# The last eight slots laid out along TensorE's list, a second exponential tile, and one-by-one projects for the last four batches

## The chip, the cores and the metric

One core of one Trainium2 chip. The time is the device time of one launch in microseconds; a number for a kernel is the median of its runs. All runs told here are of the state fast. The kernel before takes 2411.36 us (median of 4, 2406.54 to 2418.76), so differences of a few us in 2400 are near the scatter between runs. I therefore also use a length inside one trace, the **tail**: from the start of the attend of batch 116 on TensorE to the end of the span. Up to that attend the order of work is the same in all kernels here (some have one extra transfer shortly before); where it starts moved between 2250 and 2268 us from trace to trace. The tail itself repeated within 0.5 us in the two kernels that were traced twice. But in the traces of runs b, e and h one stretch of it ran at the lower clock after a gap that the other traces with list and tile passed at full pace, and the tail is about 2 us longer for it (shown under run b). So for an edit that acts only near the end I also count from the start of the attend of batch 124 on TensorE.

## The reference, cut to what matters

Two layers over x of 128 batches x 128 rows x 512 columns, all float32. The change concerns the end of the second:

```python
qkv = (h @ w_qkv)                                   # h = relu(layernorm(x))
attn = softmax(where(mask == 0, -inf, q @ k.T * scale))
o = (attn @ v) @ w_proj + b_proj
x = x + o + (layernorm(o) * gamma + beta)           # per row of 512
```

## The kernel before: the parts concerned

All work of a batch is put on a heap with a time in us on a plan of slots (17.8 us a batch), then built in order of these times. Each engine executes its instructions in that order. So a time in the plan is only a rank: it decides who stands behind whom.

```python
def softmax_exp(i, t, s, shift):
    e = work.tile([P, Q, H, R], F32, name="e", bufs=1)         # one tile for all batches
    sm = stat.tile([P, H], F32, name="sm")
    ...                                                        # 8 exponentials on ScalarE, in two halves
    put(t + 4.2, softmax_divide, i, t + 4.2, e, sm)

def softmax_divide(i, t, e, sm):
    nc.vector.reciprocal(sm, sm)
    nc.gpsimd.tensor_tensor(e, e, sm..., op=ALU.mult)
    S[i] = work.tile([P, Q, H * R], F32, name="sx", bufs=1)    # where it comes back
    exchange(max(t + 5, read_at(i)), S[i], e...)               # to DRAM and back, then a transpose

def finish_last(i, n, x1):
    nc.gpsimd.tensor_tensor(n, n, x1, op=ALU.add)
    nc.sync.dma_start(out=out[i], in_=n)                       # same SP queue as the exchanges
```

The qkv product (four batches at once) and the project (two at once) are done with 7 products in place of 8: "Q" and "p" below are one step of each. The factors for them are sums made on GpSimd (osum, hsum). A finish of a batch is: statistics on VectorE, a power on GpSimd (rs), a shift on VectorE, the normalization on ScalarE, then two more 128x512 instructions on GpSimd besides an add of the residual, and a store.

In the old plan the last batches follow rules of distance: scores of the last four 8.5 us apart, attend 22 us later, seven project steps 1.4 us apart after that.

## Time and profile before

| | before |
|---|---|
| median | 2411.36 us |
| tail | 154.0 us (2257.7 to 2411.7) |

What TensorE does in this tail is taken apart in the prediction. In the waits' view a line reads: engine, its line of the kernel, what released it, then us in total, times, longest. One line that the prediction leans on and does not show, from ScalarE's waits in the tail of the kernel before:

```profile
ACT e L409 <- DMA d<-e: 15.1, 3, 8.4
```

The exponentials waited 15.1 us in three places for their tile to leave for DRAM.

### The profile page before, as it was taken

What the parts mean: (1) busy time and instruction counts of PE and PEld (TensorE: products, weight loads), DVE (VectorE), ACT (ScalarE), POOL (GpSimd) and SP (SyncE); (2) the same over time, 40 slices, a digit from 0 to 9 for tenths busy, and PEclk for the clock granted to TensorE, in tenths of its full rate; (3) what the DMA queues carried; (4) which work ended last, traced back from release to release, by engine and by line L of the source; (5) the groups of instructions that cost most, each with busy time, mean ns of one, the idle gap of its engine ahead of it and who ended that gap; (6) DMA issues with size and microseconds to landing.
All of it is one profiled execution on the core that took longest, in us unless ns stands there. A gap on an engine that the chain in (4) does not pass through costs nothing.

```text
span 2411.7 us, 42673 instructions
## 1 busy us (share of the span) xinstructions
PE 2341.9 (97%) x14097; PEld 2052.3 (85%) x14097; DVE 1612.0 (67%) x3231; ACT 1044.3 (43%) x3074; POOL 1677.9 (70%) x1598
## 2 busy tenths in 40 slices
PE   7899999999999999999999999999999999999985
PEld 6788888888888888888888888888888888888873
DVE  5566676676676776676676676676676666766554
ACT  2344444444444444444444444444444444444332
POOL 4467677677677677677777677767777766776556
PEclk9999999999999999999999999999999999999997
DMA  7776766766766776767776776776766767676643
GB/s 233 237 230 217 231 216 215 236 218 214 232 218 220 225 223 220 225 209 227 224 226 215 231 222 206 229 221 214 235 216 218 226 209 226 218 220 212 219 153 105
DMA packets 399788, 524.10 MB, mean 217 GB/s; under 512 B 40016, under 2 KB 250064, under 8 KB 399568
## 3 DMA queue, kind: packets, MB, share of 16 engines
q1 hardware_dynamic: 398192, 519.99, 67.7%
q8 instruction: 113, 1.85, 0.3%
q10 hardware_dynamic: 1376, 1.38, 0.2%
q14 instruction: 107, 0.88, 0.1%
HBM read 350.29 MB, written 170.92 MB: 216 GB/s over the span
## 4 chain that ended last, share of the span: by engine, by line
PE 84%; DMA 5%; POOL 3%; DVE 3%; issue 2%; SPq 2%; ACT 1%; POOLq 0%; DVEq 0%; ACTq 0%
PE pc L366 37%; PE pd L286 23%; PE pz L366 6%; PE ps L386 5%; PE po L433 5%; PE pmix L272 4%; PE pz L286 4%; DMA sx<-d 2%; SPq L211 1%; DMA wq<-wt 1%; DVE pT L424 1%; POOL x1b L454 1%; POOL t L460 1%; POOL t L464 1%; DMA wq<-in_L_gnn_w_qkv_dram 1%
## 5 line engine op out<-in xcount | busy, mean ns | idle before, releaser
L193 POOL TENSOR_TENSOR rs<-ve,minus_half 128x2 f32<-128x2 f32 x192 | 134.9, 703 | 630.1 <-DVE ve L191 550.5
L366 PE MATMUL pc<-hsum,wq 128*128 128x256 f32 x2048 | 487.0, 381 | 16.2 <-ACT qkT L370 5.0
L409 ACT ACTIVATE e<-s,mx 128x128 f32<-128x128 f32 x1024 | 397.0, 389 | 194.7 <-DVE mx L400 113.2
L366 PEld LDWEIGHTS pc<-hsum,wq 128*128 128x128 f32 x2048 | 390.1, 191 | 73.6 <-ACT qkT L370 7.7
L286 PE MATMUL pd<-wp_sb,osum 128*128 128x256 f32 x1024 | 266.4, 384 | 6.9 <-DVE o L292 3.6
L418 POOL TENSOR_TENSOR e<-e,sm 128x1024 f32<-128x1024 f32 x128 | 244.9, 1913 | 36.0 <-DVE sm L417 30.7
L366 PE MATMUL pc<-h1T,wq 128*128 128x256 f32 x1024 | 246.4, 384 | 0.6 <-DMA wq<-in_L_gnn_w_qkv_dram 0.6
L286 PE MATMUL pd<-w_sb,ysum 128*128 128x256 f32 x960 | 246.3, 379 | 0.0
L366 PE MATMUL pc<-wq,hsum 128*128 128x256 f32 x1024 | 244.6, 382 | 0.0
L614 ACT COPY oT<-po 128x512 f32<-128x512 f32 x128 | 74.9, 585 | 385.2 <-PE po L433 385.2
L424 DVE STREAM_TRANSPOSE pT<-sx 128x1024 f32<-128x1024 f32 x128 | 158.5, 1238 | 124.5 <-DMA sx<-d 124.5
L286 PEld LDWEIGHTS pd<-wp_sb,osum 128*128 128x128 f32 x1024 | 191.8, 193 | 33.4 <-POOL osum L220 5.5
L366 PEld LDWEIGHTS pc<-h1T,wq 128*128 128x128 f32 x1024 | 192.9, 191 | 30.4 <-DMA wq<-in_L_gnn_w_qkv_dram 0.7
L366 PEld LDWEIGHTS pc<-wq,hsum 128*128 128x128 f32 x1024 | 191.8, 190 | 28.8
L394 DVE TENSOR_TENSOR s<-ps,maskb 128x512 f32<-128x512 f32 x256 | 159.2, 684 | 57.6 <-PE ps L386 57.6
L286 PEld LDWEIGHTS pd<-w_sb,ysum 128*128 128x128 f32 x960 | 177.9, 190 | 21.7
L370 ACT COPY qkT<-pc 128x512 f32<-128x512 f32 x256 | 144.1, 574 | 119.3 <-PE pc L366 119.1
L459 ACT ACTIVATE t<-o,shift,rs 128x512 f32<-128x512 f32 x128 | 103.1, 807 | 207.0 <-DVE shift L197 206.0
L409 ACT ACTIVATION_READ_ACCUMULATOR e<-s,mx 128x1 f32 x1024 | 191.6, 187 | 0.0
L454 POOL TENSOR_TENSOR x1b<-x1b,o 128x512 f32<-128x512 f32 x128 | 162.7, 1271 | 35.5 <-DMA x1b<-x1d 33.4
L292 DVE TENSOR_TENSOR o<-pd,bp_b 128x256 f32<-128x256 f32 x256 | 106.3, 415 | 108.1 <-PE pd L286 107.7
L188 DVE BATCH_NORM_STATS2 st<-x 128x6 f32<-128x512 f32 x256 | 172.1, 672 | 3.0 <-DMA x<-in_x_dram 2.9
(93 smaller groups left out, 4711.7 us busy)
## 6 DMA issues: line engine op xcount, KB each, us to landing
wq<-wt SPq DMA_DIRECT2D x384, 256.0 KB, 3.8
wq<-in_L_gnn_w_qkv_dram SPq DMA_DIRECT2D x288, 256.0 KB, 3.5
d<-e SPq DMA_DIRECT2D x128, 512.0 KB, 2.9
sx<-d SPq DMA_DIRECT2D x512, 128.0 KB, 2.9
x<-in_x_dram SPq DMA_DIRECT2D x128, 256.0 KB, 4.3
d<-h SPq DMA_DIRECT2D x128, 256.0 KB, 2.9
x1d<-x SPq DMA_DIRECT2D x128, 256.0 KB, 3.1
h1x<-d SPq DMA_DIRECT2D x512, 64.0 KB, 2.3
```

The costliest lines, as they stand in the source:

```text
L188: nc.vector.bn_stats(st, src)
L193: nc.gpsimd.tensor_tensor(rs, ve, minus_half, op=ALU.pow)
L286: nc.tensor.matmul(p[:, 0, :], lhsT=left[k][:, c, :], rhs=w_sb[:, k, c, :], start=first and c == 0, stop=last and c == 1, skip_group_check ...
L366: nc.tensor.matmul(p[:, half, :], lhsT=lhsT, rhs=rhs, start=first and half == 0 and c == 0, stop=last and c == 1, skip_group_check=True)
L370: nc.scalar.copy(results[n], p)
L386: nc.tensor.matmul(ps[e][:, c, :], lhsT=qk[r, c, j % 2, :], rhs=qk[r, C + c, j % 2, :], start=True, stop=True)
L394: nc.vector.tensor_tensor(s[:, e * C:(e + 1) * C, :], ps[e], m4, op=ALU.add)
L409: nc.scalar.activation(e[:, :, h, :], s[:, h, :].rearrange("p (q r) -> p q r", q=Q), AF.Exp, bias=shift[:, h:h + 1], scale=scale, accum_ou ...
L418: nc.gpsimd.tensor_tensor(e, e, sm.unsqueeze(1).unsqueeze(3).to_broadcast([P, Q, H, R]), op=ALU.mult)
L424: nc.vector.transpose(PT[i].rearrange("p h (q r) -> p q h r", q=Q), S.pop(i).rearrange("p q (h r) -> p q h r", h=H))
L433: nc.tensor.matmul(p[e * HD:(e + 1) * HD, c, :], lhsT=v[:, h:h + HD], rhs=PT[i][:, e * C + c, :], start=True, stop=True)
L454: put(t + 1 + 3 * n, lambda i=i: nc.gpsimd.tensor_tensor(X1B[i], X1B[i], O[i], op=ALU.add))
```

## The change

Its intent: let TensorE's list of the last eight slots be written down as a string (a = attend, s = scores, Q, p = steps, D = one whole project), let all other times follow from it, bring the softmaxes closer together, give odd batches a second tile for the exponentials and the way back (a free h1T buffer), and project the last four batches one by one, which needs no sums. The residual of the last eight batches is also reloaded into the six input tiles, which are free by then (not in the cut below).

```diff
+    def spare(i):
+        return i > LATE and i % 2
+    def late(n):                                  # two halves of one free h1T buffer
+        ...
     def softmax_exp(i, t, s, shift):
-        e = work.tile([P, Q, H, R], F32, name="e", bufs=1)
+        e = late(0) if spare(i) else work.tile([P, Q, H * R], F32, name="e", bufs=1)
...
-        S[i] = work.tile([P, Q, H * R], F32, name="sx", bufs=1)
+        S[i] = late(1) if spare(i) else work.tile([P, Q, H * R], F32, name="sx", bufs=1)
...
+    def project_whole(i, t):                      # 8 matmul calls, no factor sums
+        p = whole(OT, i, lambda row, col: wp_b12 if (row, col) == (0, 1) else wp_sb[...])
...
+    LATE = LAST - G
+    for key in ("aassQQpQpQpQpQppQp" "aassQQpQpQpQpQppQpQQQQQ" "aassQpQppQp" "aassppQp" "QpQppQpppp"
+                "aaD" "aaDDD"):
+        AT[key].append(t)
+        t += dict(a=0.9, s=0.9, Q=1.73, p=0.87, D=3.46)[key]
...
     def softmax_at(i):
+        return TAIL + (5, 13, 26, 35, 58, 63.5, 70.5, 76)[i - LATE]
     def read_at(i):
+        return TAIL + (16, 24, 37, 46, 69, 74.5, 81.5, 87)[i - LATE]
...
+    put(when(LATE - 1, 6), nc.sync.dma_start, wp_b12, block(w_proj, 0, F))
```

More of the change, by code (lines that the diff above doesn't have):

```diff
@@ L68 @@
     ctx.enter_context(tc.manual_schedule())
+    LATER = []
     X, H0, YT, X1, X1D, H1, H1T, WQ, QKT, V, S, PT, OT, O, X1B, LEFT0, LEFT1, LEFT2 = ({} for _ in range(18))
@@ L179, in make_mask, with stats_of @@
         nc.vector.tensor_scalar(maskb, edge, some, None, op0=ALU.add)
-    def stats_of(pair):
-        mv = stat.tile([P, 2, nc.vector.BN_AGGR_DIM], F32, name="mv")
-        for n, src in enumerate(pair):
+    def stats_of(srcs):
+        w = len(srcs)
+        mv = stat.tile([P, 2, nc.vector.BN_AGGR_DIM], F32, name="mv")[:, :w]
+        for n, src in enumerate(srcs):
             st = stat.tile([P, nc.vector.BN_STATS_DIM], F32, name="st")
@@ L189, in stats_of @@
             nc.vector.bn_aggr(mv[:, n], st)
-        ve = stat.tile([P, 2], F32, name="ve")
+        ve = stat.tile([P, 2], F32, name="ve")[:, :w]
         nc.vector.tensor_scalar(ve, mv[:, :, 1], EPS, None, op0=ALU.add)
-        rs = stat.tile([P, 2], F32, name="rs")
-        nc.gpsimd.tensor_tensor(rs, ve, minus_half, op=ALU.pow)
-        shift = stat.tile([P, 2], F32, name="shift")
+        rs = stat.tile([P, 2], F32, name="rs")[:, :w]
+        nc.gpsimd.tensor_tensor(rs, ve, minus_half[:, :w], op=ALU.pow)
+        shift = stat.tile([P, 2], F32, name="shift")[:, :w]
         def shifts():
             nc.vector.scalar_tensor_tensor(shift, mv[:, :, 0], -1.0, rs, op0=ALU.mult, op1=ALU.mult)
-        return shifts, [dict(bias=shift[:, n:n + 1], scale=rs[:, n:n + 1]) for n in range(2)]
+        return shifts, [dict(bias=shift[:, n:n + 1], scale=rs[:, n:n + 1]) for n in range(w)]
     def exchange(t, dst, src):
@@ L296, in layer0_whole @@
     def layer0_whole(i, t):
-        p = psum.tile([P, 2, F], F32, tag=f"d{i % 2}", name=f"pd{i % 2}", bufs=1)
-        y = YT[i // 2] if i % 2 == 0 else YT.pop(i // 2)
-        for c in range(C):
-            for col in range(2):
-                nc.tensor.matmul(p[:, col, :], lhsT=y[:, c, i % 2, :], rhs=w0_sb[:, BLOCKS[c // 2][col], c % 2, :],
-                                 start=c == 0 and col == 0, stop=c == C - 1, skip_group_check=True)
+        p = whole(YT, i, lambda row, col: w0_sb[:, BLOCKS[row][col]])
         X1[i] = work.tile([P, D], F32, name="x1", bufs=3)
-        put(t + 3.6, lambda: nc.vector.tensor_tensor(X1[i], p.rearrange("p a f -> p (a f)"), X.pop(i), op=ALU.add))
+        put(t + 3.6, nc.vector.tensor_tensor, X1[i], p, X.pop(i), ALU.add)
     def layer0(j):
@@ L401, in softmax_max @@
         put(t + 1.4, softmax_exp, i, t + 1.4, s, mx)
+    def spare(i):
+        return i > LATE and i % 2
+    def late(n):
+        if not LATER:
+            t = work.tile([P, C, G, P], F32, name="h1T").rearrange("p (n c) j m -> p n (c j m)", n=2)
+            LATER.extend(t[:, n].rearrange("p (q w) -> p q w", q=Q) for n in range(2))
+        return LATER[n]
     def softmax_exp(i, t, s, shift):
-        e = work.tile([P, Q, H, R], F32, name="e", bufs=1)
+        e = late(0) if spare(i) else work.tile([P, Q, H * R], F32, name="e", bufs=1)
+        e = e.rearrange("p q (h r) -> p q h r", h=H)
         sm = stat.tile([P, H], F32, name="sm")
@@ L443, in project, with whole, finish @@
         return pair_chain(LEFT2.pop(j), wp_sb, (O[2 * j], O[2 * j + 1]), (bp_b, bp_b), "d1", "d0")
+    def whole(src, i, rhs):
+        p = psum.tile([P, 2, F], F32, tag=f"d{i % 2}", name=f"pd{i % 2}", bufs=1)
+        y = src[i // 2] if i % 2 == 0 else src.pop(i // 2)
+        for c in range(C):
+            for col in range(2):
+                nc.tensor.matmul(p[:, col, :], lhsT=y[:, c, i % 2, :], rhs=rhs(c // 2, col)[:, c % 2, :],
+                                 start=c == 0 and col == 0, stop=c == C - 1, skip_group_check=True)
+        return p.rearrange("p a f -> p (a f)")
+    def project_whole(i, t):
+        p = whole(OT, i, lambda row, col: wp_b12 if (row, col) == (0, 1) else wp_sb[:, BLOCKS[row][col]])
+        O[i] = work.tile([P, D], F32, name="o", bufs=4)
+        put(t + 3.6, nc.vector.tensor_tensor, O[i], p, bp_b, ALU.add)
     def reload(i):
-        X1B[i] = work.tile([P, D], F32, name="x1b", bufs=2)
+        X1B[i] = work.tile([P, D], F32, name="x", bufs=6) if i >= LATE else work.tile([P, D], F32, name="x1b", bufs=2)
         nc.sync.dma_start(out=X1B[i], in_=X1D.pop(i))
-    def finish(j, t):
-        pair = 2 * j, 2 * j + 1
-        shifts, args = stats_of([O[i] for i in pair])
+    def finish(batches, t):
+        shifts, args = stats_of([O[i] for i in batches])
         put(t + 3, shifts)
-        for n, (i, arg) in enumerate(zip(pair, args)):
+        for n, (i, arg) in enumerate(zip(batches, args)):
             put(t + 1 + 3 * n, lambda i=i: nc.gpsimd.tensor_tensor(X1B[i], X1B[i], O[i], op=ALU.add))
@@ L506, in run @@
             put(t, step, t, k)
+    LATE = LAST - G
+    AT = {key: [] for key in "asQpD"}
+    t, last = when(LATE, 0), ""
+    for key in ("aassQQpQpQpQpQppQp" "aassQQpQpQpQpQppQpQQQQQ" "aassQpQppQp" "aassppQp" "QpQppQpppp"
+                "aaD" "aaDDD"):
+        AT[key].append(t)
+        t += dict(a=0.9, s=0.9, Q=1.73, p=0.87, D=3.46)[key]
+        t += 0.2 * (key != last and "a" in (key, last) or key != last and "s" in (key, last))
+        last = key
+    TAIL = when(LATE, 0)
     def scores_at(i):
-        if i < LAST:
-            return when(i - i % 2, 2 + i % 2)
-        return when(LAST, 2) + (i - LAST) * 8.5
+        return when(i - i % 2, 2 + i % 2) if i < LATE else AT["s"][i - LATE]
     def softmax_at(i):
-        if i < LAST and i % 2:
-            return when(i, 0.5)
-        return scores_at(i) + 3
+        if i < LATE:
+            return when(i, 0.5) if i % 2 else scores_at(i) + 3
+        return TAIL + (5, 13, 26, 35, 58, 63.5, 70.5, 76)[i - LATE]
     def read_at(i):
-        return when(i + 1, 9) if i < LAST and i % 2 else 0
+        if i < LATE:
+            return when(i + 1, 9) if i % 2 else 0
+        return TAIL + (16, 24, 37, 46, 69, 74.5, 81.5, 87)[i - LATE]
     def flip_at(i):
-        if i < LAST:
+        if i < LATE:
             return when(i + 1, 15) if i % 2 else when(i + 2, 7.4)
-        return scores_at(i) + 20.5
+        return TAIL + (27, 29.5, 56, 58, 73, 78.5, 89.3, 91)[i - LATE]
     def attend_at(i):
-        if i < LAST:
-            return when(min(i - i % 2 + 4, LAST + 1), i % 2)
-        return scores_at(i) + 22
-    def stage(t, f, n, *a, bound=B):
-        if 0 <= n < bound:
-            put(t, f, n, *a)
+        return when(i - i % 2 + 4, i % 2) if i < LATE - 4 else AT["a"][i - LATE + 4]
     PAIR = ((5.6, 8.2, 10.8, 12.5, 15.0, 15.9, 18.5), (3.2, 5.8, 8.4, 10.1, 12.7, 13.5, 16.1))
@@ L545 @@
         put(attend_at(i), attend, i, attend_at(i))
-    idle = when(LAST, 13)
     for j in range(B // 2):
@@ L572 @@
         t = attend_at(b) + 2
-        put(t, pair_left, j, t, 3.4 if i < LAST else 1, OT, LEFT2, "osum")
-        if i < LAST:
-            times = [when(i, p) for p in PAIR[1]]
-            end = when(i + 1, 1.2)
-        else:
-            times = [max(t, idle) + 1 + k * 1.4 for k in range(7)]
-            idle = times[6] + 1
-            end = times[6] + 2
-        run(lambda j=j: project(j), times)
-        put(end - 7, reload, a)
-        put(end - 4, reload, b)
-        put(end, finish, j, end)
+        if b < LAST:
+            put(t, pair_left, j, t, 3.4 if i < LATE else 1.5, OT, LEFT2, "osum")
+            n = 7 * (a - LATE + 4) // 2
+            times = [when(i, p) for p in PAIR[1]] if i < LATE else AT["p"][n:n + 7]
+            run(lambda j=j: project(j), times)
+            ends = [((a, b), when(i + 1, 1.2) if i < LATE else times[6] + 2.2)]
+        else:
+            ends = []
+            for n in (a, b):
+                t = AT["D"][n - LAST]
+                put(t, project_whole, n, t)
+                ends.append(((n,), t + 4.6))
+        for batches, t in ends:
+            for n in batches:
+                put(t - 7 + 3 * (n % 2), reload, n)
+            put(t, finish, batches, t)
     steps = []
@@ L588 @@
         i = g * G - 3
-        t = when(i - 1, 13) if g else START + 36.2
-        put(t, group_left, g, t, 4 if g else 1.4)
+        t, gap = (START + 36.2, 1.4) if g == 0 else (when(i - 1, 13), 4) if i < LATE else (TAIL + 9.8, 2.2)
+        put(t, group_left, g, t, gap)
         times = sorted(when(i + n, p) for n in range(G) for p in GROUP[(i + n) % 2] + ((13.1,) if n == 0 else ()))
+        if i + G > LATE:
+            n = sum(t < TAIL for t in times)
+            times[n:] = AT["Q"][:5] if g == LATE // G else AT["Q"][5:]
         for kind in KINDS:
@@ L600 @@
     for kind, (t, tiles) in enumerate((
-            (START + 25, (("sx", 1, [P, Q, H * R]), ("pT", 2, [P, 2 * C, P]), ("s", 2, [P, 2 * C, P]), ("e", 1, [P, Q, H, R]))),
+            (START + 25, (("sx", 1, [P, Q, H * R]), ("pT", 2, [P, 2 * C, P]), ("s", 2, [P, 2 * C, P]), ("e", 1, [P, Q, H * R]))),
             (START + 37, (("pT", 2, [P, 2 * C, P]), ("s", 2, [P, 2 * C, P])) + (("o", 4, [P, D]),) * 4),
@@ L610 @@
     put(when(2, 12), combine_square, nc.gpsimd, wp_sb)
+    wp_b12 = w0_sb[:, 1]
+    put(when(LATE - 1, 6), nc.sync.dma_start, wp_b12, block(w_proj, 0, F))
     while later:
```

## The prediction

> **What bounds the kernel now.** I read the busy shares first, then the chain that ended last, then TensorE's timeline and wait table over the part that the change touches, then the timelines of GpSimd and of the SP queue there. The page's first part:
>
> ```profile
> PE 2341.9 (97%) x14097; PEld 2052.3 (85%) x14097; DVE 1612.0 (67%) x3231; ACT 1044.3 (43%) x3074; POOL 1677.9 (70%) x1598
> ```
>
> TensorE is busy 97% of the span, so the body of the kernel cannot gain from a new order of work. What is left is the end. The busy time by stretch (columns: length, then busy us and count of PE, PEld, DVE, ACT, POOL, then granted clock, DMA share, GB/s) shows where TensorE stops being full:
>
> ```profile
> 2187.00:2257.00 70.00, 70.00 (x423) 61.55 (x423) 44.69 (x89) 28.67 (x90) 44.07 (x41) 1.00 0.67 212
> ...
> 2257.70:2411.70 154.00, 115.88 (x697) 93.60 (x696) 77.74 (x149) 50.96 (x169) 93.62 (x85) 0.89 0.47 149
> ```
>
> Before 2257 it is busy 70 of 70 us; after it 115.9 of 154, at a clock of 0.89. The boundary is the attend of batches 116 and 117, where the last eight slots begin. In TensorE's timeline there the reader is to see the gaps in brackets, and the same four matmul records lasting 2.04 us after a gap instead of 1.03:
>
> ```profile
> 2303.78 5.45 PE L366 MATMUL pc<-hsum,wq 128*128 128x256 f32 x24 [3.35 <-ACT qkT L370]
> ...
> 2340.09 2.04 PE L286 MATMUL pd<-wp_sb,osum 128*128 128x256 f32 x4 [3.08 <-DVE o L292]
> ...
> 2386.97 1.98 PE L433 MATMUL po<-pT,v 128*64 128x128 f32 x16 [6.62 <-DVE pT L424]
> ...
> 2396.98 1.03 PE L286 MATMUL pd<-wp_sb,oT 128*128 128x256 f32 x4
> ```
>
> TensorE's waits from 2257.7 on:
>
> ```profile
> PE po L433 <- DVE pT L424: 10.5, 3, 6.6
> PE pc L366 <- ACT qkT L370: 5.0, 2, 3.4
> PE pd L286 <- DVE o L292: 4.2, 3, 3.1
> PE pd L286 <- POOL osum L220: 3.2, 2, 2.5
> PE pc L366 <- DVE v L249: 1.5, 1, 1.5
> ```
>
> They sum to 24.4 us. The account of the tail of 154.0 us is then: busy 115.9, waits 24.4, and 13.7 after the last matmul ends at 2398.0. At full clock the work would take less than 115.9. By the rows of this timeline, one attend takes 0.95 us, one batch of scores 1.0, one step of the qkv product (Q, eight records) 1.73, one step of a project pair (p, four records) 0.865. The tail holds 12 attends, 8 scores, 26 Q and 42 p: 11.4 + 8 + 45.0 + 36.3 = 100.7. So about 15 us of busy time is the lower clock.
>
> **What the Trainium skill says.** "TensorE: Matmul & The Clock Gate", part 1, says that the array falls to half its rate after an idle window of about 3.4 us and returns after such a window of work. The trace agrees in kind: 2.04 against 1.03 us for the same four records, after gaps of 3.08 and 6.62. (A gap of 3.35 at 2303.78 cost nothing, so a gap of that length need not.) "PSUM — Partial Sum Buffer", section "Engine vs sequencer instructions", calls the queues of ScalarE, VectorE and GpSimd strict FIFO; so one instruction that waits holds up all behind it, and the rows of each engine here start in the program's order. "DMA: Bandwidth & Descriptors", in its section on the anatomy of one DMA, says that a wait of a transfer is held on the issuing sequencer; in this trace the SP queue spends 45.9 us of the tail waiting to issue stores of the result, and later transfers stand behind it. Its fixed cost of about 2 us fits what one leg of the exchange through DRAM takes here, 2.6 to 3.5 us.
>
> **The change part by part.** Up to the attends at 2257.7 the built order of all engines is the same in both kernels, apart from one extra transfer of a weight block shortly before. So I predict only what follows, in us from 2257.7.
>
> 1. TensorE's list. The last pairs' project steps are now laid between the qkv steps of group 31. Two of the six pairs (14 p, 12.1 us) become four whole projects D of 8 calls, 3.46 us each (a Q holds 4 calls in 1.73): 28 p are left. Sum: 11.4 + 8 + 45.0 + 24.2 + 13.8 = 102.4 us, 1.7 more than before. In exchange these four need no factor sums on GpSimd (2 pairs x 4 x 0.72 = 5.8 us less) and finish one batch at a time.
>
> 2. The exchange behind each softmax. Measured pieces: scores 1.0, mask 1.25, maximum and its scaling 1.5, exponentials 3.2, reciprocal 0.3, multiply 1.9 on GpSimd, then out to DRAM 3.0, four issues 1.8, landing 2.9, transpose 1.25: 18.1 us from scores to attend. With one exponential buffer this stood in series; the wait of the exponentials for their transfer is 15.1 us in three places. The second pair of buffers for odd batches removes that. In the new list scores and attend are 52.8, 43.4, 33.7 and 24.9 us apart for the four pairs (for the last: the list is at 65.3 at the attends before those scores and at 90.2 at their attend), so on paper all four exchanges fit.
>
> 3. What still stalls TensorE, walking the new order of each engine with these durations. (a) The third qkv step of a kind on bank x waits for ScalarE's copy; at 30.2 ScalarE is held by a normalization that waits for VectorE's shift (29.0), then four exponentials, then copies at 31.9: about 1.8 us. (b) Two steps near 74 and 82 wait for VectorE behind a reciprocal and a transpose: 1.0 and 0.7. (c) The last one is the large one. The multiply of batch 127 ends near 88.6. On the SP queue its transfer out is followed by two stores of results that wait for GpSimd's adds (89.8 and 92.3), and only then by the transfers back. These go out at 93 to 95 and land near 98; the transpose ends near 99. TensorE reaches that attend near 94.8: a stall of 4.4 us. Projects 125 to 127 stand behind it and end near 110.5: 102.4 + 7.9.
>
> 4. The end. One instruction over 128x512 on GpSimd costs 1.23 us start to start, and a finish needs three and a power of 0.68: 4.4 us against 3.46 of a D. VectorE's statistics of batch 124 stand behind the late transpose, so GpSimd is held until about 101. From there its list has 4 powers and 15 instructions: 2.7 + 18.5 = 21.2, ending at 122.2. TensorE's own end would allow about 116: 110.5 + add, statistics and aggregate 1.8, power 0.7, shift 0.3, normalization 0.8, multiply and add 2.5. So GpSimd sets the end. From its last add to the end of the span took 3.1 us before (2408.6 to 2411.7): 125.3.
>
> Sum: 154.0 - 125.3 = 28.7 us less, which is +1.7 of work, -16.5 of waits, about -15 of low clock (nearly all, since gaps become short), and the drain after the last matmul 14.8 instead of 13.7. 2410.6 - 28.7 = 2381.9; I say 2382.
>
> **The rivals.** First: the plan holds and the stall of 4.4 is not there. Then TensorE ends near 105 and GpSimd, not held, near 118: end 121, time 2378. For it speaks that the gaps in the list were laid out with room; against it the 45.9 us of SP waiting for GpSimd's adds before, and that the same stores still stand ahead of the last exchange. Second: the waits return on another engine. GpSimd had 93.6 us of work in 154; it now has about 89 (5.8 less for sums, 1.4 more for two extra powers) in 125, and the second exponential tile makes each instruction on it wait for ScalarE's previous one in the built program. If each softmax of an odd batch is 2 to 3 us later and the clock falls again for one window in the last projects, the end is at 133 to 136: 2390 to 2393. Third: the extra weight block or the reused input buffers delay a qkv weight in the body. The DMA share of 0.67 there leaves room, and the block is 256 KB in 2411 us; at most 1 us. A gain of over 2% would need an end at 106, less than 4 us after 102.4 us of pure matmul work, while the last finish alone takes over 9 us: that can be excluded but for noise.
>
> **Range and chances.** The walk's end of 125.3 is uncertain by some 5 us either way (gaps on one side, a second low-clock window on the other), and the runs of before spread over 12 us. I take 2372 to 2394, and faster by over 2% 0.02, within 2% 0.97, slower 0.01.
>
> **What would show it.** TensorE's busy time after 2257.7 falls from 115.9 to 103 to 107; its waits from 24 to about 8, the longest for the transpose of batch 127 just ahead of the last attend, with the SP queue waiting for GpSimd's add just before; the clock of the last hundred us is above 0.93; the wait of exponentials for the transfer out of their tile is nearly gone; the chain ends in GpSimd's normalizing lines, almost without pause over the last 20 us; the span before 2257.7 is unchanged. I am wrong if the span ends above 2395 with waits for qkv copies or weights in the middle, or if the last exchange is early and the chain ends through TensorE.

## The result, and the profile after

The changed kernel takes 2390.77 us (median of 4, 2387.51 to 2391.66) against 2411.36. The ratio of the fast runs is 0.991, with an interval from 0.9882 to 0.9937. (A ratio is the mean time of one kernel's fast runs over that of the other's of the same rounds, so not quite the ratio of the medians.) At the bound of 2% this counts as the same; it is 20.6 us less, clear of noise. The prediction said 2382, range 2372 to 2394.

The page's first part, and the busy time by stretch, of the changed kernel:

```profile
PE 2335.9 (98%) x14105; PEld 2052.5 (86%) x14105; DVE 1604.7 (67%) x3225; ACT 1044.4 (44%) x3074; POOL 1674.3 (70%) x1592
```

```profile
2187.00:2257.00 70.00, 69.97 (x421) 61.06 (x420) 45.08 (x89) 28.64 (x90) 45.42 (x43) 1.00 0.68 216
2257.70:2388.10 130.40, 108.37 (x712) 92.69 (x710) 75.94 (x143) 50.89 (x169) 89.10 (x79) 0.95 0.56 178
```

The body is as before, the end has a clock of 0.95 instead of 0.89. Here the attend of 116 starts at 2259.27, so the tail is 2388.1 - 2259.3 = 128.8 us. TensorE's waits in the tail:

```profile
PE po L440 <- DVE pT L431: 4.3, 1, 4.3
PE pd L288 <- DVE o L294: 2.4, 2, 1.6
PE pc L362 <- POOL t L481: 1.8, 1, 1.8
```

24.4 us have become 8.5, ScalarE's 15.1 us of waiting for the transfer out of the exponentials' tile are gone from its waits, and half of what is left is one wait, for the transposed probabilities of batch 127. In TensorE's timeline:

```profile
2291.73 1.97 PE L362 MATMUL pc<-hsum,wq 128*128 128x256 f32 x8 [1.79 <-POOL t L481]
...
2339.74 1.13 PE L288 MATMUL pd<-wp_sb,oT 128*128 128x256 f32 x4 [1.64 <-DVE o L294]
...
2361.36 1.68 PE L440 MATMUL po<-pT,v 128*64 128x128 f32 x16 [4.29 <-DVE pT L431]
2362.96 1.22 PE L458 MATMUL pd<-wp_sb,oT 128*128 128x256 f32 x2
2363.98 1.06 PE L458 MATMUL pd<-w_sb,oT 128*128 128x256 f32 x2
...
2368.00 0.59 PE L458 MATMUL pd<-w_sb,oT 128*128 128x256 f32 x2
```

The first of these waits is put down to GpSimd (L481), but that instruction had ended at 2291.21. What ended just before TensorE went on is ScalarE's copy out of an accumulator, at 2291.63:

```profile
2291.07 0.56 ACT L366 COPY qkT<-pc 128x512 f32<-128x512 f32 x1
```

After the gap of 4.29 us the same pair of records lasts 1.06 instead of 0.59: this is the only gap in the tail that was followed by a slow stretch. GpSimd's timeline at the end, where the first line's mark is its longest pause there, the last line its last instruction:

```profile
2363.09 0.56 POOL L195 TENSOR_TENSOR rs<-ve,minus_half 128x1 f32<-128x1 f32 x1 [4.86 <-DVE ve L193]
...
2383.81 1.26 POOL L485 TENSOR_TENSOR t<-t,x 128x512 f32<-128x512 f32 x1
```

TensorE's last matmul ends at 2374.6 and GpSimd's last add at 2385.1; the drain is 13.5 us.

### The profile page after: what moved, and what is told of

Its sections match the earlier page's. It is cut to its first block, busy times and chain, and to the rows that moved or that the text cites. A ratio compares the mean times of both kernels' runs of the same rounds, so it can differ in the third digit from the quotient of the medians.

```text
span 2388.1 us, 42653 instructions
## 1 busy us (share of the span) xinstructions
PE 2335.9 (98%) x14105; PEld 2052.5 (86%) x14105; DVE 1604.7 (67%) x3225; ACT 1044.4 (44%) x3074; POOL 1674.3 (70%) x1592
## 4 chain that ended last, share of the span: by engine, by line
PE 84%; DMA 6%; DVE 4%; POOL 3%; SPq 2%; issue 2%; ACT 1%; POOLq 0%; DVEq 0%; ACTq 0%
PE pc L362 37%; PE pd L288 24%; PE pz L362 6%; PE ps L382 5%; PE po L440 5%; PE pmix L274 4%; PE pz L288 4%; DMA sx<-d 2%; SPq L213 1%; DVE pT L431 1%; DMA wq<-in_L_gnn_w_qkv_dram 1%; DMA h1x<-d 1%; POOL t L481 1%; DMA wq<-wt 1%; ACT e L416 1%
## 5 line engine op out<-in xcount | busy, mean ns | idle before, releaser
L195 POOL TENSOR_TENSOR rs<-ve,minus_half 128x2 f32<-128x2 f32 (+1 forms) x194 | 136.0, 701 | 614.7 <-DVE ve L193 520.6
L416 ACT ACTIVATE e<-s,mx 128x128 f32<-128x128 f32 x992 | 384.6, 389 | 180.6 <-DVE mx L396 114.8
L425 POOL TENSOR_TENSOR e<-e,sm 128x1024 f32<-128x1024 f32 x124 | 237.5, 1915 | 32.1 <-DVE sm L424 26.8
L288 PE MATMUL pd<-wp_sb,osum 128*128 128x256 f32 x992 | 254.4, 379 | 0.7 <-DVE o L294 0.7
L431 DVE STREAM_TRANSPOSE pT<-sx 128x1024 f32<-128x1024 f32 x124 | 153.4, 1237 | 128.8 <-DMA sx<-d 126.7
L288 PEld LDWEIGHTS pd<-wp_sb,osum 128*128 128x128 f32 x992 | 184.0, 190 | 23.8 <-POOL rs L195 1.1
L416 ACT ACTIVATION_READ_ACCUMULATOR e<-s,mx 128x1 f32 x992 | 185.7, 187 | 0.0
L475 POOL TENSOR_TENSOR x1b<-x1b,o 128x512 f32<-128x512 f32 x120 | 152.7, 1273 | 35.4 <-DMA x1b<-x1d 31.9
L481 POOL TENSOR_TENSOR t<-t,gamma_b 128x512 f32<-128x512 f32 x128 | 163.1, 1274 | 10.7 <-ACT t L480 10.7
```

The source lines that it names most:

```text
L195: nc.gpsimd.tensor_tensor(rs, ve, minus_half[:, :w], op=ALU.pow)
L288: nc.tensor.matmul(p[:, 0, :], lhsT=left[k][:, c, :], rhs=w_sb[:, k, c, :], start=first and c == 0, stop=last and c == 1, skip_group_check ...
L416: nc.scalar.activation(e[:, :, h, :], s[:, h, :].rearrange("p (q r) -> p q r", q=Q), AF.Exp, bias=shift[:, h:h + 1], scale=scale, accum_ou ...
L425: nc.gpsimd.tensor_tensor(e, e, sm.unsqueeze(1).unsqueeze(3).to_broadcast([P, Q, H, R]), op=ALU.mult)
L431: nc.vector.transpose(PT[i].rearrange("p h (q r) -> p q h r", q=Q), S.pop(i).rearrange("p q (h r) -> p q h r", h=H))
L475: put(t + 1 + 3 * n, lambda i=i: nc.gpsimd.tensor_tensor(X1B[i], X1B[i], O[i], op=ALU.add))
```

## The experiments

All are checked against the reference and gave correct results. The table has the tail of each trace and what it is made of; "busy", "waits" and "drain" are TensorE's busy time, its waits, and the time after its last matmul. They add up to the tail within 0.3 us (gaps under 0.15 us are not listed as waits). The expectations were written before each run. Runs a to d shared one chip (before: 2417.03 us there), e to h another visit (2408.18), i to l a third (2413.18).

```
run                  median   ratio   95%               tail   busy   waits  drain
before               2411.36  -       -                 154.0  115.9  24.4   13.7
changed              2390.77  0.991   0.9882 to 0.9937  128.8  106.8   8.5   13.5
a one tile           2412.84  0.9986  0.9973 to 0.9999  151.5  115.4  22.8   13.3
b pairs at the end   2394.79  0.9921  0.9907 to 0.9934  132.9  108.5   9.6   14.6
c list only          2416.16  1.0003  0.9994 to 1.0012  155.5  115.8  25.8   13.6
d tile only          2416.56  1.0001  0.9988 to 1.0015  155.8  115.9  26.1   13.7
e store later        2384.03  0.9899  0.9883 to 0.9915  130.7  109.7   7.7   13.3
f early 127          2379.33  0.9879  0.9862 to 0.9896  123.8  105.2   4.7   13.9
g adds on VectorE    2383.53  0.9897  0.9881 to 0.9913  126.9  106.8   8.8   11.1
h f and g            2383.10  0.9888  0.9866 to 0.9910  123.8  106.8   4.4   12.5
i second e only      2398.07  0.9933  0.9909 to 0.9957  135.7  109.9  12.5   13.3
k changed again      2392.28  0.9907  0.9885 to 0.9928  129.3  107.6   8.3   13.3
l f again            2385.44  0.9879  0.9859 to 0.9899  124.1  105.2   5.0   13.8
```

The runs a to d take the change apart. My theory when I sent them was that the order along TensorE's list brings most of the gain; the rival was the second tile. "Order" here is the list with all times that follow from it, and the reload into the input tiles; these were not varied apart.

**a. One tile.**

```diff
     def spare(i):
-        return i > LATE and i % 2
+        return False
```

> The changed kernel with the second exponential tile taken back: even and odd batches share one pair of buffers again. The tail is counted from the start of the attend of batch 116 to the end of the span; it was 154.0 us before (2257.7 to 2411.7) and 128.8 after (2259.3 to 2388.1). My theory, that the order along TensorE's list brings most of the gain: the exponentials of odd batches wait again for the transfer out, batch 127 comes 4 to 6 us later, tail 132 to 136. Rival, that the second tile brings most of it: tail above 143. If the tile is worth nothing: 128 to 130.

Measured: tail 151.5. Nearly the whole gain is gone, and the rival's number (above 143) holds. ScalarE's timeline of this run shows how:

```profile
2346.10 0.40 ACT L416 ACTIVATE e<-s,mx 128x128 f32<-128x128 f32 x1 [9.95 <-DMA d<-e]
...
2347.66 1.04 ACT L366 COPY v<-pc 128x512 f32<-128x512 f32 x2
...
2350.15 1.05 ACT L648 COPY oT<-po 128x512 f32<-128x512 f32 x2
```

An exponential stands 9.95 us for the transfer out of its tile. Behind it in ScalarE's queue stand the copies that empty TensorE's accumulators: those of the attends that ended at 2342.4 come only at 2350.15. So TensorE waits as well, by its waits in the tail of this run:

```profile
PE ps L382 <- ACT oT L648: 7.3, 1, 7.3
...
PE pc L362 <- DMA wq<-in_L_gnn_w_qkv_dram: 3.7, 1, 3.7
```

**b. Pairs at the end.** The last four batches as two pairs, each with its sums.

```diff
-    "aaD" "aaDDD"
+    "aaDD" "aaDD"            # D only keeps the place in the plan
-        if b < LAST:
+        if True:             # and for b > LAST: seven steps 0.87 apart from attend + 2.4
```

> The changed kernel with the last four batches projected as two pairs again (7 steps and four sums on GpSimd each) in place of four whole projects. TensorE has 1.7 us less work, and the first pair's steps fill the stall ahead of the attend of 127; against that the second pair waits for sums on GpSimd and finishes two at a time. My estimate from the pieces: tail 126 to 131, that is, the one-by-one projects are worth within 3 us of nothing. Rival, that they brought a good part of the gain: tail above 134.

Measured: tail 132.9, a miss by 2 us above my range and below the rival's 134. The tail is 132.9 - 128.8 = 4.1 us longer. TensorE's waits in it:

```profile
PE pd L288 <- POOL osum L222: 4.6, 3, 3.0
PE pc L362 <- POOL t L481: 2.6, 1, 2.6
```

The first line, the waits for sums, is what the whole projects avoid; the stall of 4.3 us ahead of the attend of 127 is gone in return. The second line is not theirs. It is the gap of 1.79 us shown above, which all kernels with list and tile have, and in this trace the matmuls after it ran slowly. The same eight records, in b, in h, and in k (the changed kernel again):

```profile
2290.58 3.61 PE L362 MATMUL pc<-hsum,wq 128*128 128x256 f32 x8 [2.65 <-POOL t L481]
```

```profile
2290.39 3.60 PE L362 MATMUL pc<-hsum,wq 128*128 128x256 f32 x8 [2.01 <-POOL t L481]
```

```profile
2288.43 1.97 PE L362 MATMUL pc<-hsum,wq 128*128 128x256 f32 x8 [2.13 <-POOL t L481]
```

So b reaches the attend of 124 at 93.2 us of its tail, the changed kernel at 91.2 (91.0 in k), though b's edit acts only after it. From that attend to the end it is 39.7 us in b against 37.7 (38.3 in k): by this count the whole projects are worth about 2 us, within the 3 that I expected, and the rest of the 4.1 is not theirs.

**c. The list only**, both edits at once.

> Both taken back at once: the new order of TensorE's list and of the softmaxes alone, one exponential tile, last two pairs as pairs. If the order is the cause: tail 130 to 137, so at least 17 of the 25 us stay. If the gain needs the tile or the whole projects: tail above 143.

Measured: tail 155.5 and a ratio of 1.0003. The new list with one tile is worth nothing at all: my theory that the order alone is the cause has fallen.

**d. The tile only**: the second pair of buffers in the kernel before, with its order.

> The kernel before with the second pair of exponential buffers alone, old order. The exponentials waited 15.1 us for the transfer out in three places there, the attends 10.5 us for their transpose. My theory: with the old order only some of this is on the path, tail 146 to 152. Rival, that the tile is the main part: tail below 142. Nothing: 153 to 155.

Measured: tail 155.8, ratio 1.0001. So the rival falls too, and my range of 146 to 152 was missed: the tile without the list is worth nothing either. (The 1.8 us over the kernel before lie ahead of the attend of 118, where a qkv weight comes 1.7 us late; from there on both take 120.9.) ScalarE's wait for the transfer out is gone in this run, and TensorE's waits are the old ones:

```profile
PE po L444 <- DVE pT L435: 10.4, 3, 6.6
PE pc L367 <- ACT qkT L371: 5.4, 2, 3.4
```

From the tails: before 154.0, list alone 155.5, tile alone 155.8, list and tile (b) 132.9, with the whole projects 128.8. Two parts that are each worth nothing are worth 21 us together. In the old order nothing uses a tile that is free early. The first exponential of batch 127 in the kernel before, then in run d with the scaling of the maximum that it needs:

```profile
2361.85 0.40 ACT L409 ACTIVATE e<-s,mx 128x128 f32<-128x128 f32 x1 [3.31 <-DMA d<-e]
```

```profile
2361.93 0.40 ACT L420 ACTIVATE h1T<-s,mx 128x128 f32<-128x128 f32 x1 [3.11 <-issue]
```

```profile
2361.09 0.76 DVE L401 TENSOR_SCALAR mx<-mx 128x8 f32<-128x8 f32 x1
```

With a free tile they start only 0.1 us earlier, counted from the attend of 118, because the maximum on VectorE is ready only then; those of 123 start 0.4 us earlier. Those of 125 start 4.5 us earlier, but their multiply only 1.0, and the transpose, which keeps its place in VectorE's list, not at all (70.7 us after that attend before, 70.8 in d). In the new order the softmaxes of two batches follow so closely that the second one's exponentials meet an occupied tile, and in ScalarE's queue that wait is passed on to TensorE (run a). By the tails the projects are worth 4.0 us without the tile (155.5 - 151.5); from the attend of 124 on it is 5.0 without it and, as said, about 2 with it.

**i. Which half of the tile.** The second tile for the exponentials only; what returns from DRAM lands in the one old tile.

```diff
-        S[i] = late(1) if spare(i) else work.tile([P, Q, H * R], F32, name="sx", bufs=1)
+        S[i] = work.tile([P, Q, H * R], F32, name="sx", bufs=1)
```

> The changed kernel with the second tile used for the exponentials alone: what comes back from DRAM for odd batches lands in the one old tile again. Taking both halves away cost nearly the whole gain (tail 151.5 instead of 128.8). If the exponentials' half is what matters (ScalarE held by the transfer out): tail 128 to 133. If the landing half matters as much (the transfers back wait on the SP queue until the even batch is transposed, which itself waits for an attend, with the qkv weights behind them): tail 138 to 150.

Measured: tail 135.7, between the two numbers. Of the 22.7 us between a and the changed kernel, the exponentials' half is worth 15.8 and the landing half, added to it, 6.9; the landing half alone was not run. The second shows on the SP queue, which waits to issue a transfer back until the other batch has been transposed, and in a qkv weight that comes late behind it (the SP queue's waits, then TensorE's):

```profile
SPq L213 <- DVE pT L431: 8.0, 3, 7.5
```

```profile
PE pc L362 <- DMA wq<-in_L_gnn_w_qkv_dram: 4.1, 1, 4.1
```

The runs e to h test what the prediction said of the last stall and of the end.

**e. Stores later.** The stores of results 120 and 121 are issued after the last transfers back.

```diff
-        nc.sync.dma_start(out=out[i], in_=n)
+        if i in (LATE, LATE + 1):
+            put(TAIL + 88, nc.sync.dma_start, out[i], n)
+        else: ...
```

The prediction laid the stall ahead of the attend of 127 on these stores. The SP queue of the changed kernel already says how much they can do (start, length, line of an issue):

```profile
2349.89 0.34 SPq L208 DMA_DIRECT2D d<-h1T  x1
2351.12 0.36 SPq L486 DMA_DIRECT2D out_dram<-t  x1
...
2353.70 0.34 SPq L486 DMA_DIRECT2D out_dram<-t  x1
...
2354.82 1.80 SPq L213 DMA_DIRECT2D h1T<-d  x4
```

> The changed kernel with the stores of results 120 and 121 issued after the last transfers back, so that these no longer stand behind them on the SP queue. In the trace of the changed kernel the transfer out of batch 127 was issued at 2349.9 and the transfers back at 2354.8, so the stores can have held them by 1.6 to 2 us only. From that: the stall ahead of the attend of 127 falls from 4.3 to about 2.5 us, tail 126.5 to 128.5 (128.8 in the changed kernel). The prediction's reading, that the stores make this stall: it falls below 1 us, tail 124 to 125.5.

Measured, in TensorE's timeline: the stall falls from 4.29 to 2.78, as I expected from these lines, not to below 1.

```profile
2355.30 1.98 PE L440 MATMUL po<-pT,v 128*64 128x128 f32 x16 [2.78 <-DVE pT L431]
```

The tail, 130.7, did not follow: this trace lost 2.4 us ahead of the attend of 124 (93.5 us after the start of the tail instead of 91.2), where the edit does nothing: it is the slow stretch shown under b, here after a gap of 2.77 us. From that attend to the end it is 37.2 us, against 37.7 in the changed kernel and 38.3 in k. So 0.5 to 1.0 of the 1.5 us reached the end, hardly more than these two traces of one kernel differ.

**f. An early maximum.** The transfer out of 127 was late because its multiply was late. VectorE's timeline of the changed kernel shows where the time was lost:

```profile
2334.56 0.42 DVE L251 TENSOR_TENSOR o<-pz,o 128x256 f32<-128x256 f32 x1
2337.54 1.25 DVE L431 STREAM_TRANSPOSE pT<-sx 128x1024 f32<-128x1024 f32 x1 [2.56 <-DMA sx<-d]
...
2339.61 1.20 DVE L395 TENSOR_REDUCE mx<-s 128x8 f32<-128x1024 f32 x1
```

The transpose of batch 124 waits 2.56 us for its data; the maximum of 127, whose data are there, stands behind it. The edit puts it ahead:

```diff
-        return TAIL + (5, 13, 26, 35, 58, 63.5, 70.5, 76)[i - LATE]
+        return TAIL + (5, 13, 26, 35, 58, 63.5, 70.5, 72.6)[i - LATE]
-        return TAIL + (16, 24, 37, 46, 69, 74.5, 81.5, 87)[i - LATE]
+        return TAIL + (16, 24, 37, 46, 69, 74.5, 81.5, 82)[i - LATE]
```

> The changed kernel with the maximum of batch 127 on VectorE ahead of the transpose of batch 124 (which sat 2.6 us waiting for its transfer, with the maximum behind it), and the transfers back of 127 ahead of one of the two stores. If the stall of 4.3 us comes from this late softmax: the stall is gone, the low clock after it too, GpSimd is held until about 2358 instead of 2363, tail 123 to 125.5. Rival, that GpSimd's own amount of work sets the end whatever TensorE does: tail 127.5 to 129.

Measured: tail 123.8, and the stall is 0.38:

```profile
2348.66 1.09 PE L440 MATMUL po<-pT,v 128*64 128x128 f32 x16 [0.38 <-DVE pT L431]
```

Here GpSimd never pauses from 2349 to its last add at 2371.2, and TensorE has ended at 2360.3: with the stall gone, GpSimd's own list still sets the end. The edit does two things at once, since the transfers back of 127 also come ahead of one of the stores. The trace says what each is worth: counted in the tail, the multiply of 127 ends at 86.6 us instead of 90.6, and its transfers back go out at 90.9 instead of 95.6. So 4.0 of the 4.7 us are the earlier softmax.

**g. Adds on VectorE.** The residual add of the last four batches moves from GpSimd to VectorE.

```diff
-  nc.gpsimd.tensor_tensor(X1B[i], X1B[i], O[i], op=ALU.add)
+  (nc.vector if i >= LAST else nc.gpsimd).tensor_tensor(X1B[i], X1B[i], O[i], op=ALU.add)
```

> The changed kernel with the residual add of the last four batches on VectorE in place of GpSimd. If GpSimd sets the end: four times 1.23 us less on its list, then the end is TensorE's plus 6.2 and 3.0: tail 123.5 to 126. Rival, that VectorE holds the adds for the reloaded tiles and with them the statistics behind: tail 128 or more.

Measured: tail 126.9, 0.9 above my range; the drain is 11.1 instead of 13.5. The direction holds, the size does not: four adds of 1.23 us are 4.9, and 1.9 were gained (2.3 from the attend of 124 on, 35.4 against 37.7).

**h. Both.**

> Both edits, the early maximum of 127 and the adds on VectorE. If both causes are as I read them they add up: TensorE ends 6 us earlier, GpSimd's list after the hold is 16.3 us: tail 117 to 121. If they overlap (either one uncovers the same bound): 123 to 125. If it is the sum it is a kernel that beats both, 2379 to 2384 us against 2390 of the changed kernel.

Measured: tail 123.8, as in f. By the tail they do not add up. But this trace lost about 2 us in the slow stretch shown under b, after its gap of 2.01 us: it reaches the attend of 124 at 93.1 us instead of f's 91.3, where neither edit acts. From that attend to the end it is 30.7 us, against 32.6 in f and 37.7 in the changed kernel; the 7.0 gained there are near the sum of f's 5.1 and g's 2.3. So the two edits do nearly add up. The median of h, 3.8 us above that of f, does not show it. Part of why g and h give less than the four adds promise can be read off: in both, GpSimd's powers last 0.93 to 1.01 us where the changed kernel and f have 0.55 to 0.57. From run h, GpSimd's power and the VectorE add that runs at the same time, then the same power in f:

```profile
2359.10 0.98 POOL L195 TENSOR_TENSOR rs<-ve,minus_half 128x1 f32<-128x1 f32 x1
```

```profile
2358.94 0.72 DVE L475 TENSOR_TENSOR x<-x,o 128x512 f32<-128x512 f32 x1
```

```profile
2357.15 0.57 POOL L195 TENSOR_TENSOR rs<-ve,minus_half 128x1 f32<-128x1 f32 x1
```

Four powers at 0.4 more are 1.6 of the 3 us that g lacks. The Trainium skill says this on the page "GPSIMD Engine Reference", section "Specifications": GpSimd's ways into SBUF are shared with VectorE, and contended by VectorE instructions with two SBUF inputs. The add is one; the trace agrees, with 0.98 against 0.57. All eight slow powers of g and h run beside such an add, and the power of 0.57 in f runs beside a VectorE add that takes one of its inputs from TensorE's accumulators (o<-pd,bp_b).

**k and l. Head to head.** The changed kernel and f again, on one chip.

> The changed kernel once more, on the same chip as the next, as a control. Tail 128.8 in its first trace; between traces the attend of 116 moved between 2250 and 2268 us with the same order of work, so I expect a tail of 127 to 131 and a total that moves by up to 8 us with the body.

> The early maximum of batch 127 once more, beside the changed kernel on one chip. Its tail was 123.8 against 128.8. If that is the edit's: tail 123 to 125 and a total 3 to 7 us, 0.1 to 0.3%, below the changed kernel's of the same rounds. If its better total was the chip's: no difference in total.

Measured: tails 129.3 and 124.1; medians 2392.28 and 2385.44, 6.8 us apart, ratios to the kernel before 0.9907 and 0.9879. The intervals of the two ratios overlap, so the total alone does not settle it; the tail, twice 5.0 to 5.2 us shorter, does; that is more than the 2.4 us that e lost to the slow stretch and its gap, and none of these four traces has that stretch. Version f beats both kernels.

## Why the prediction was right or wrong

The time lay in the range, 9 us above the point. Of these 9 us the tail explains 3.5 (128.8 instead of 125.3).

**Where TensorE waits: right, in part by luck.** It named three places. (a) 1.8 us for a copy on ScalarE: measured 1.79. (b) 1.0 and 0.7: measured 1.64 and 0.74. (c) 4.4 ahead of the attend of 127: measured 4.29. Together 7.9 against 8.5. Not all of this is foresight. For (a) the mechanism came as told, the copy behind four exponentials (it was expected to start at 31.9 and started at 31.8). For (b) the two steps came at 80.5 and 84.9 instead of near 74 and 82, the first behind a transpose that waited 2.56 us for its transfer (shown under f), the second behind the statistics of a pair; a reciprocal and a transpose had been named. And the length of (c) came out so near because both of its ends came 3 us late: TensorE reached that attend at 97.8 instead of 94.8, and the transpose ended at 102.0 instead of 99.

Three of the prediction's sums are a little off, and nothing hangs on them: 102.4 + 7.9 is 110.3 and not 110.5, the pieces added to it make 116.6 and not 116, and by its own durations the third pair's room is 32.0 and not 33.7. Also, this room is counted from the attends ahead of the scores; from the scores it is 1.9 us less, still over 18.1 for every pair.

**The reason for (c): half wrong.** The step "On the SP queue its transfer out is followed by two stores ..., and only then by the transfers back" is true in the trace but is 1.5 us of the stall (run e). The larger part is the late softmax of 127, caused by a transpose that waits on VectorE ahead of its maximum (run f). With the stall gone the tail is 123.8, not the 121 of the first rival.

**TensorE's own time: the mis-sized term.** The sum took 102.4 us of work at full clock; measured busy is 106.8. Of these 4.4 us, the timeline shows about 1.2 as 0.1 us at each of some twelve changes between attends, scores and the other kinds (0.96 from the start of a p to an attend in the kernel before, where 0.865 was taken), 0.8 inside the scores of 126 and 127 (2.90 instead of 2.06, which need accumulators that ScalarE frees late), and 1.7 after the stall at the lower clock; 0.7 is left over. Up to the attend of 127 the sum had 2.5 us of work and 0.7 of waiting too little, so TensorE came there about 3 us late, and with it all that follows. "Nearly all" of the 15 us of low clock going away was right; the clock of the last hundred us, expected above 0.93, came out as 0.94 (0.95 over the tail).

**GpSimd sets the end: right, 3 us later.** "Held until about 101" was 103.8 us (2363.09 - 2259.27), since the transpose of 127, and behind it the statistics of 124, came 3.0 us later than laid out; from there 22.0 us instead of 21.2, with one further pause of 1.1; the last 3.0 as before. This makes 128.8 instead of 125.3. In run f, TensorE ended 14 us before the span and GpSimd did not pause.

**The rival on the second tile: wrong.** It feared 2 to 3 us per odd softmax, because each exponential waits for the one before. Exponentials in both tiles start 0.38 to 0.40 us apart; the waits cost nothing.

**What brings the gain: not told apart.** The prediction credited the removed waits to the tile and the list together; its step 2 said that on paper the exchanges fit. So it was right on the total by a sum that did not ask which part would do it. My theory for the runs, the list, was wrong, and so was its rival: neither is worth anything alone.

**The rest of the total is open.** By the traces the tail is 25.2 us shorter, the medians differ by 20.6 (and 20.9 in run k). The body started its tail at 2257.7 in one trace and 2259.3 and 2255.6 in two others; the interval of the ratio, 0.9882 to 0.9937, is 15 to 28 us and holds both. Whether the extra weight transfer costs the body anything was not measured.

## What to carry to other kernels

A closer order of work and a second buffer can each be worth nothing and only together be worth something: try them together before dropping either. On engines that execute in order, look at what stands behind a wait, not only at the wait; here an exponential held by a transfer stopped the copies behind it and with them TensorE, and a transpose waiting for its data held a maximum that was ready. At the end of a kernel count the work of each engine from the moment it is last held: GpSimd's list set the end after TensorE had finished. And before a length in one trace is credited to an edit, look where in the trace the time was lost: b, e and h each lost about 2 us in a stretch that their edits do not touch.

## What the Trainium skill lacked or had wrong

- "TensorE: Matmul & The Clock Gate", part 1, ties the lower clock to an idle window of about 3.4 us. Here gaps of 3.08 us (kernel before) and 2.01 us (run h), too short to hold such a window, were followed by records at half pace (2.04 us instead of 1.03, 3.60 instead of 1.97), while gaps of 3.35 us (kernel before) and 2.13 us (run k) were followed by matmuls at full pace. So in these traces the length of a gap between 2 and 3.4 us does not tell.
- "GPSIMD Engine Reference" has no duration for a power: here one over 128x1 took 0.55 to 0.57 us, and 0.93 to 1.01 us beside VectorE adds with two SBUF inputs.
- "TensorEngine Tiling (Array Packing)" gives no number for a change between tile shapes on TensorE; here it cost about 0.1 us each time (0.96 from the start of a project step, `128*128`, to an attend, `128*64`, where such steps alone follow at 0.865).
